# Score tiles off the diagonal by seven half-size products, in one fused graph-layer kernel

## The chip, the cores and the metric

The kernel runs on one core of a Trainium2 chip. Times are device microseconds (us) of one launch. The core has TensorE (PE in the profile, with its weight loads listed as PEld), VectorE (DVE), ScalarE (ACT), GpSimd (POOL) and SyncE (SP). POOL and SP are used here almost only to issue DMA transfers. Each engine has its own queue and takes its instructions in the order of that queue; engines wait for each other through semaphores.

## The reference

Two graph layers on x (4096 rows, 512 columns) with an adjacency matrix adj (4096 x 4096, sparse, symmetric in its pattern). Cut to what matters:

```
ba = maximum(sign(x), 0);  bw = sign(W0)
x  = layernorm(x + relu(adj @ (ba @ bw.T)))          # layer 0

node_att = softmax(x @ node_w, axis=0)               # layer 1
h        = x @ edge_w
e        = h @ h.T                                   # 4096 x 4096 scores, fp32
edge_att = softmax(where(adj > 0, e, -9e15), axis=1)
out      = (adj * (node_att * edge_att)) @ (x @ W1) + bias
x        = layernorm(x + out)
```

The scores e are symmetric, so a tile of e and its transpose are the same numbers. They are products in full fp32.

## The kernel before, in words

P is 128, W is 512. The 4096 rows are eight groups of 512 (index A for the rows of a score tile, B for its columns); h is kept transposed in SBUF as hT (contraction in KD = 4 slices of 128).

**Four stages follow each other.** Layer 0 runs from 0 to about 560 us. h is computed up to 602 us (function `seven`). The score stage runs from 602 to 1063 us. It computes e tile by tile, masks it, takes each row's minimum of the negated scores (VectorE, line 669), the exponentials and their row sums (ScalarE, line 678), and stores the raw scores to HBM in both orientations. From 1063 us to the end the aggregation multiplies the weights that belong to the scores with x (class `Aggregate`, matmuls at line 1326) and finishes with W1 and the layernorm (`Finish`).

**The score stage** is a list `runs` (lines 1636 to 1641). It holds `Single` tiles of 512 x 512, and runs of `Couple`s. There are eight Singles on the diagonal (A equal to B, upper triangle only), four off it, (2,3), (4,5), (0,1) and (6,7), and twelve Couples of 512 x 1024. Together they cover each unordered pair of groups once. `Mirror.turn` (line 707) makes the transposed tile with four TensorE transposes for each block of 128 rows, and ScalarE copies them out of PSUM (line 708).

- A `Single` off the diagonal computes each of its four row blocks with four fp32 matmuls of 512 columns (line 745) into one PSUM bank, which ScalarE copies to SBUF (line 755). There are six such banks in the queue `banks`.
- A `Couple` replaces eight half-size block products by seven, in the way of Strassen and Winograd. It forms sums and differences of quarters of hT on VectorE (`operands`, lines 781 to 813), and products into PSUM (`quad`, line 924), which ScalarE copies (lines 948, 953, 961, 966) or VectorE adds up (line 962). Two of its seven products are again made by seven smaller ones (`second` at line 846, `third` at line 883).

**What sets the order.** In this stage the program text gives a first order: `between()` is called within the tiles, and `tick` takes at most a few deferred jobs from three queues (`turns`: transposes; `stats`: row minima and stores; `exps`: exponentials). Then the tile scheduler is free to reorder instructions on each engine by its own estimates. Only in the aggregation is the order of TensorE, VectorE and ScalarE fixed by hand (`manual_schedule`).

**Buffers.** `free` holds tiles of 128 x 2048 fp32, `free_h` fourteen halves of other such tiles (masks, strips of scores, operands), `free_s` a single tile (slot5; every second Couple's left sums), `lopp` four tiles of 128 x 1024 (a run's right operands, later the left operands of the aggregation). `take` forces deferred jobs when a store is empty.

**The end of the stage.** Seven Singles follow the last run. While they run (`closing`), `early_steps` of the first aggregation block are started between their matmuls: two mask loads, the shifts (line 1095), exponentials (line 1098) and weights (line 1111) of four tiles. After the last Single the differences of these tiles (lines 1120 to 1128) and the first aggregation products follow.

**The end of a run of Couples.** Lines 1710 to 1716 let the last Couple's `third` (four steps, `tail_`) take turns with the last two steps of its second `quad` (`rest_`).

Of the kernel before, what the change touches and what calls it, by code (L numbers as in the profile page):

```python
# [11 lines left out]
F32 = mybir.dt.float32  # L12
# [6 lines left out]
P = 128  # L19
# [10 lines left out]
def kernel(  # L30
# [13 lines left out]
    nc = tc.nc  # L44
    N, D = x.shape
    NB = N // P
    KD = D // P
    W = 512
    NG = N // W
    BG = W // P  # L50
# [675 lines left out]
    class Single:  # L726
# [7 lines left out]
        def main(self, between):  # L734
            A, B = self.A, self.B
            s = Uses(BG + 1 if self.diag else 3 * BG)
            if self.diag:
                self.mirror.t = s
            elif self.stays:
                kept_tiles[A, B] = s.buf  # L740
            for i in range(BG):
                lo = i if self.diag else 0
                pe = banks.popleft()
                for k in range(KD):
                    nc.tensor.matmul(  # L745
                        pe[:, lo * P :],
                        hT[:, k, ts(A * BG + i, P)],
                        hT[:, k, (B * BG + lo) * P : (B + 1) * W],
                        start=(k == 0),
                        stop=(k == KD - 1),  # L750
                    )
                    if k == KD - 1 or k % 2 and not (self.diag and i > 1):
                        between()
                src = s.buf[:, i, :]
                nc.scalar.copy(src[:, lo * P :], pe[:, lo * P :])  # L755
                banks.append(pe)
                turns.append((now[0] + 3, lambda i=i, s=s, src=src: self.mirror.turn(s, src, i)))
                if not self.diag:
                    stats.append((self.here.ready, 1, lambda i=i, s=s, src=src: self.here.row(i, s, src)))

                    if self.stays:
                        continue

                    def store(i=i, s=s, src=src):
                        nc.gpsimd.dma_start(s_d[A][B // 2][:, i, B % 2, :], src)
                        s.used()

                    stats.append((at_once, 0, store))

    class Couple:  # L770
        right, inner_right = {}, {}
# [9 lines left out]
        def operands(self):  # L781
            A, B, h = self.A, self.B, KD // 2
            if B not in Couple.right:
                r11, r12 = (hT[:, :h, ts(c, W)] for c in (B, B + 1))
                r21, r22 = (hT[:, h:, ts(c, W)] for c in (B, B + 1))
                t1, t2, t3, t4 = (lopp.tile([P, h, W], F32, name="right", tag="lop") for _ in range(4))
                nc.vector.tensor_sub(t1, r12, r11)
                nc.vector.tensor_sub(t2, r22, t1)
                nc.vector.tensor_sub(t3, r22, r12)
                nc.vector.tensor_sub(t4, r21, t2)  # L790
                Couple.right[B] = r11, r21, r22, t4, t1, t2, t3
                Couple.inner_right[B] = self.second_right(r21), self.second_right(r22)
            low, high = (hT[:, f : f + h, ts(A, W)].rearrange("p k (q u w) -> p k q u w", u=2, w=P) for f in (0, h))
            l11, l21 = (low[:, :, :, u, :] for u in range(2))
            l12, l22 = (high[:, :, :, u, :] for u in range(2))
            Couple.made[0] += 1
            self.sums = None
            if Couple.made[0] % 2:
                s2, s1, s3, s4 = (rows.tile([P, h, 2, P], F32, name="left", tag="rows") for _ in range(4))
            else:  # L800
                self.sums = Uses(1, free_s)
                s2, s1, s3, s4 = (
                    self.sums.buf[:, n, :].rearrange("p (k q w) -> p k q w", k=h, w=P) for n in range(4)
                )
            nc.vector.tensor_add(s1, l21, l22)
            nc.vector.tensor_sub(s2, s1, l11)
            nc.vector.tensor_sub(s3, l11, l21)
            nc.vector.tensor_sub(s4, l12, s2)
            self.left = l11, l12, s4, l22, s1, s2, s3
            self.inner_sums = Uses(2, free_h)  # L810
            self.inner_left = [self.second_left(l, n) for n, l in enumerate((l12, s4))]
            self.rows11, self.rows12, self.zs = [None] * 2, [None] * 2, [None] * 2
            self.written = [None] * 2
# [456 lines left out]
    class Sums:  # L1270
# [34 lines left out]
        def multiply(self):  # L1305
            r, m = self.unit.r, self.m
            if self.begin:
                lops["lop"] = lopp.tile([P, BG, HD], F32, name="lop")
                nc.sync.dma_start(lops["lop"], lop_d[r][:, m])
            if self.begin and self.ns:  # L1310
                lops["inner"] = lopp.tile([P, BG // 2, 4, P], F32, name="lop2", tag="lop")
                nc.sync.dma_start(lops["inner"], lop2_d[r][:, SPLIT.index(m)])
            if self.ns:
                products = []
                for k, n in enumerate(self.ns):
                    if n in (2, 4, 5, 6):
                        lop = lops["inner"][:, :, n - 3 if n > 2 else 0, :]
                    else:
                        lop = lops["lop"][:, 2 * (n > 0) :, P * (n > 1) :][:, : BG // 2, :P]
                    products.append((self.bank[:, ts(k, W // 2)], lop, self.unit.halves[n], BG // 2))  # L1320
            else:
                products = [(self.bank, lops["lop"][:, :, ts(self.h, P)], self.unit.right(m), BG)]
            start = self.fresh and self.w == W
            for ps, lop, rop, K in products:
                for k in range(K):
                    nc.tensor.matmul(ps, lop[:, k, :], rop[:, k, :], start=start, stop=(k == K - 1), skip_group_check=True)  # L1326
                    start = False
            spend("pe", 0.43 * self.work)
            self.done = clock["pe"]
            if self.keep:  # L1330
                kept.append(self.bank)
# [301 lines left out]
    def couples(B, *As):  # L1633
        return [Couple(A, B) for A in As]

    runs = [Single(2, 2), Single(2, 3), couples(4, 2, 3, 0, 1)]
    runs += [Single(4, 4), Single(4, 5), couples(6, 2, 3, 0, 1, 4, 5)]
    runs += [Single(3, 3), couples(2, 0, 1)]
    every = [c for u in runs if isinstance(u, list) for c in u]
    tail = len(runs)  # L1640
    runs += [Single(0, 0), Single(0, 1), Single(1, 1), Single(6, 6), Single(6, 7), Single(7, 7), Single(5, 5)]
    masks = deque(r for u in runs for c in (u if isinstance(u, list) else [u]) for r in c.masks)
    early_ = deque()

# [20 lines left out]
    for n, u in enumerate(runs):  # L1665
        unit[0] = n
        closing[0] = n >= tail
        if isinstance(u, Single):
            final = []
            u.main(between)  # L1670
            for later in runs[n + 1 : n + 3]:
                if isinstance(later, list) and later[0].left is None:
                    later[0].operands()
            continue
        final = u[-1].mirrors
        quads = [[c.quad(q, between) for q in range(2)] for c in u]
        inners = [c.second(between) for c in u]
        tails = [c.third(between) for c in u]
        for k, c in enumerate(u):
            first, second = quads[k]  # L1680
            rest_ = quads[k - 1][1] if k else None
            next(first)
            if rest_:
                tail_ = tails[k - 1]
                next(tail_)
                next(rest_)
                next(tail_)
            next(first)
            if rest_:
                next(tail_)  # L1690
            next(first)
            if rest_:
                next(rest_)
                next(tail_)
                if u[k - 1].sums:
                    u[k - 1].sums.used()
            next(first)
            inner_ = inners[k]
            next(inner_)
            next(second)  # L1700
            if k + 1 < len(u):
                u[k + 1].operands()
            next(inner_)
            next(first)
            next(inner_)
            next(second)
            next(inner_)
            next(second)
            next(inner_)
        rest_, tail_ = quads[-1][1], tails[-1]  # L1710
        next(tail_)
        next(rest_)
        next(tail_)
        next(rest_)
        next(tail_)
        next(tail_)
        if u[-1].sums:
            u[-1].sums.used()
    while turns or stats or exps:
# [145 lines left out]
```

## Time and profile before

| | us |
|---|---|
| median of 3 runs (1907.35 to 1907.94) | 1907.55 |
| the profiled execution's own time | 1908.56 |
| its span on the core | 1906.8 |
| score stage, first to last L745 matmul | 602.5 to 1062.0 |
| granted TensorE clock over the span | 0.999 of full speed |

An fp32 matmul stands in the trace as two rows, each with a weight load of its own. A row of 128x512 shows 592 ns, but the next one starts 0.43 us later, because matmuls overlap in the pipeline; so one fp32 matmul of 512 columns takes 0.86 us of TensorE. For VectorE and ScalarE too, what a row shows is a little longer than the distance to the next one when they follow each other without a wait. The number behind the bar in a row of the groups is busy time, then the mean duration in ns, then the engine's idle time just before, with what ended it.

### The profile page before, as it was taken

To read this page: it belongs to the slowest core of one execution; us is meant where nothing else is said; L and a number is where in the kernel's file an instruction comes from. 1 tells how busy PE (TensorE), PEld (TensorE's weight loads), DVE (VectorE), ACT (ScalarE), POOL (GpSimd) and SP (SyncE) were. 2 spreads that over 40 slices of the span, in tenths; PEclk is the share of its full clock that TensorE was granted. 3 is DMA by queue.
4 is the path that set the end of the run, shared out by engine and by line. 5 is a ranking of instruction groups with operands and counts; after the bars stand their busy time and mean duration, and the time that the engine had idled before them with its cause. 6 is when DMAs were issued, how large, how long until landed. Compare 5 with 4: busy or idle time off the path is not lost.

```text
span 1906.8 us, 20976 instructions
## 1 busy us (share of the span) xinstructions
PE 1893.8 (99%) x6958; PEld 1247.2 (65%) x6958; DVE 1495.8 (78%) x2357; ACT 1024.9 (54%) x1653; POOL 315.0 (17%) x449
## 2 busy tenths in 40 slices
PE   9999999999999999999999999999999999999998
PEld 6888888888644555565565556666666666656646
DVE  7777677776876588788874887898879988898947
ACT  6433333333212567566777666666676567657732
POOL 0133132231431111111110111111111101110100
PEclk9999999999999999999999999999999999999999
DMA  9889898898585379577784878877877877787731
GB/s 320 303 319 362 303 345 321 326 360 312 178 299 191 139 269 340 187 262 276 280 349 159 318 276 291 293 287 288 278 279 284 299 269 282 265 313 252 282 118 56
DMA packets 143917, 520.97 MB, mean 273 GB/s; under 512 B 15040, under 2 KB 15040, under 8 KB 136128
## 3 DMA queue, kind: packets, MB, share of 16 engines
q1 hardware_dynamic: 64368, 235.43, 36.5%
q0 software_dynamic: 67632, 248.54, 34.0%
q10 hardware_dynamic: 11808, 35.66, 5.1%
q8 instruction: 55, 0.90, 0.2%
q14 instruction: 54, 0.44, 0.1%
HBM read 397.93 MB, written 121.63 MB: 272 GB/s over the span
## 4 chain that ended last, share of the span: by engine, by line
PE 67%; issue 16%; DVE 6%; POOL 5%; DMA 2%; ACT 2%; POOLq 0%; ACTq 0%; SPq 0%; DVEq 0%
PE bank L1326 33%; PE bank L924 10%; PE bank L745 6%; PE seven L101 5%; PE po L1476 4%; PE pt L707 3%; POOL mask_d L340 2%; PE bank L883 2%; PE bank L846 2%; DVE lent L1095 1%; PE acc L253 1%; PE acc L255 1%; POOL x_d L368 1%; DMA xt<-in_x_t_dram 1%; PE bank L1476 1%
## 5 line engine op out<-in xcount | busy, mean ns | idle before, releaser
L1326 PE MATMUL bank<-slot,lop 128*128 128x256 f32 (+1 forms) x1304 | 399.9, 455 | 0.8 <-DMA lop<-lop_d 0.4
L459 PE MATMUL acc<-xw,hi 128*128 128x512 f32 x960 | 376.5, 392 | 0.0
L460 PE MATMUL acc<-xw,lo 128*128 128x512 f32 x960 | 374.3, 390 | 0.2 <-DVE lo L451 0.2
L1326 PE MATMUL bank<-lent,lop 128*128 128x512 f32 (+1 forms) x992 | 369.0, 520 | 1.2 <-DVE lent L1107 1.2
L1326 PEld LDWEIGHTS bank<-slot,lop 128*128 128x128 f32 x1304 | 247.0, 190 | 129.0 <-issue 102.6
L1326 PEld LDWEIGHTS bank<-lent,lop 128*128 128x128 f32 x992 | 188.3, 190 | 154.7 <-issue 139.7
L449 ACT CAST hi<-at 128x1024 fp32r<-128x1024 f32 x120 | 126.5, 1054 | 203.2 <-PE acc L459 149.2
L1337 ACT COPY over<-bank 128x512 f32<-128x512 f32 x200 | 116.1, 586 | 199.4 <-PE bank L1326 195.8
L460 PEld LDWEIGHTS acc<-xw,lo 128*128 128x128 f32 x960 | 180.3, 188 | 37.3 <-DVE lo L451 0.6
L459 PEld LDWEIGHTS acc<-xw,hi 128*128 128x128 f32 x960 | 180.3, 188 | 36.8
L451 DVE TENSOR_TENSOR lo<-at,hi 128x1024 fp32r<-128x1024 f32 x120 | 147.7, 1231 | 66.3 <-ACT hi L449 65.9
L745 PE MATMUL bank<-hT 128*128 128x512 f32 (+3 forms) x384 | 132.3, 486 | 0.0
L678 ACT ACTIVATE line<-line,nmax_c 128x512 f32<-128x512 f32 x160 | 115.0, 726 | 22.9 <-DVE nmax_c L669 22.6
L669 DVE CUSTOM_DVE_ANT_0 line<-lent,slot 128x512 f32<-128x512 bf16 x144 | 93.0, 687 | 40.0 <-ACT slot L755 21.7
L1488 DVE SCALAR_TENSOR_TENSOR xb<-po,f,xb 128x256 f32<-128x256 f32 x84 | 40.3, 481 | 75.0 <-PE po L1476 74.9
L745 PEld LDWEIGHTS bank<-hT 128*128 128x128 f32 x384 | 64.8, 191 | 40.5 <-issue 32.5
L1299 ACT COPY bank<-over 128x512 f32<-128x512 f32 x144 | 86.7, 603 | 0.0
L1095 DVE CUSTOM_DVE_ANT_1 lent<-lent,line 128x2048 f32<-128x2048 f32 x36 | 82.0, 2283 | 0.0
L1098 ACT ACTIVATE lent<-lent 128x2048 f32<-128x2048 f32 x36 | 69.2, 1921 | 19.0 <-DVE lent L1095 19.0
L707 PEld LDWEIGHTS pt<-ident,lent 128*128 128x128 f32 x406 | 50.7, 141 | 35.9 <-issue 24.8
L420 ACT COPY x1T<-pt 128x512 f32<-128x512 f32 x32 | 18.8, 587 | 102.3 <-PE pt L419 102.3
L708 ACT COPY slot<-pt 128x512 f32<-128x512 f32 (+3 forms) x125 | 67.8, 553 | 9.7 <-PE pt L707 9.7
(322 smaller groups left out, 3161.3 us busy)
## 6 DMA issues: line engine op xcount, KB each, us to landing
lop<-lop_d SPq DMA_DIRECT2D x154, 512.0 KB, 4.6
at<-in_adj_t_dram SPq DMA_DIRECT2D x60, 1024.0 KB, 7.1
lent<-in_adj_t_dram POOLq DMA_DIRECT2D x34, 1024.0 KB, 7.6
lent<-s_d POOLq DMA_DIRECT2D x33, 1024.0 KB, 8.2
s_d<-slot POOLq DMA_DIRECT2D x32, 1024.0 KB, 7.7
slot<-in_adj_t_dram POOLq DMA_DIRECT2D x30, 1024.0 KB, 7.9
slot<-s_d POOLq DMA_DIRECT2D x27, 1024.0 KB, 7.9
lent<-in_adj_dram SPq DMA_DIRECT2D x48, 512.0 KB, 6.2
```

The costliest lines, as they stand in the source:

```text
L101: nc.tensor.matmul(banks[bank][q], lop(m, q)[k], rop(m)[k], start=(first and k == 0), stop=(k == K - 1), skip_group_check=not first,)
L449: nc.scalar.copy(hi, aq)
L451: nc.vector.tensor_sub(lo, aq, hi.bitcast(F32))
L459: nc.tensor.matmul(acc, hi[:, c, :], xw[:, kb, :], start=(kb == 0), stop=False)
L460: nc.tensor.matmul(acc, lo[:, c, :], xw[:, kb, :], start=False, stop=(kb == NB - 1))
L678: nc.scalar.activation(line, line, AF.Exp, bias=nmax_c[:, b, c : c + 1], scale=-1.0, accum_out=sum_c[:, b, c : c + 1])
L707: nc.tensor.transpose(pt[:, j, :], src[:, ts(j, P)], ident)
L745: nc.tensor.matmul(pe[:, lo * P :], hT[:, k, ts(A * BG + i, P)], hT[:, k, (B * BG + lo) * P : (B + 1) * W], start=(k == 0), stop=(k == KD ...
L924: nc.tensor.matmul(ps, left[m][:, k, q, :], right[m][:, k, :], start=(first and k == 0), stop=(k == KD // 2 - 1), skip_group_check=not first,)
L1095: pinned[0](nc.vector._custom_dve(TENSOR_ADD_SAT, out=q, in0=q, in1=m, s0=0.0, s1=-HUGE))
L1326: nc.tensor.matmul(ps, lop[:, k, :], rop[:, k, :], start=start, stop=(k == K - 1), skip_group_check=True)
L1337: nc.scalar.copy(self.to(), self.bank[:, : self.w])
```

## The change

Class `Seventh`, a `Single`, takes the four tiles off the diagonal. It halves a 512 x 512 tile in all three directions (rows in blocks of 128 that alternate, columns in halves of 256, contraction in halves of two slices), forms four sums on the left and four on the right with eight VectorE instructions of 128x512, and makes seven products, for each of two q (a pair of row blocks): each product is two fp32 matmuls of 256 columns. For each q they share two banks, (y, z) and (u, v): half y accumulates products 0, 5 and 6, half z products 4 and 2, and u and v hold products 1 and 3. ScalarE copies y after 0, 5 and 6 and z after 4; VectorE adds u, z, y and v to the copies in SBUF.

The operands of a Seventh are formed before the Single ahead of it in the list. For (2,3) the right sums lie in two halves of `free_h`; for the others in two `lopp` tiles. The left sums lie in the one tile of `free_s` until the Seventh is done. Four stores, sixteen transposes and eight rows of statistics for a tile stay as they were.

The last hunk moves the last step of `rest_` (product 3 of the last quad of a run, 2 matmuls of 512 columns) behind the last two steps of `tail_`.

```
--- before.py
+++ after.py
@@ -767,6 +767,93 @@
 
                     stats.append((at_once, 0, store))
 
+    class Seventh(Single):
+
+        def operands(self):
+            h, w = KD // 2, W // 2
+            cols = [slice(self.B * W + n * w, self.B * W + (n + 1) * w) for n in range(2)]
+            (r11, r12), (r21, r22) = ([hT[:, f : f + h, c] for c in cols] for f in (0, h))
+            if self.A == 2:
+                self.keep = [Uses(1, free_h) for _ in range(2)]
+                both = [x.buf for x in self.keep]
+            else:
+                self.keep = []
+                both = [lopp.tile([P, h, W], F32, name="right", tag="lop") for _ in range(2)]
+            t1, t2, t3, t4 = (both[n // 2][:, n % 2, :].rearrange("p (k w) -> p k w", w=w) for n in range(4))
+            nc.vector.tensor_sub(t1, r12, r11)
+            nc.vector.tensor_sub(t2, r22, t1)
+            nc.vector.tensor_sub(t3, r22, r12)
+            nc.vector.tensor_sub(t4, r21, t2)
+            self.right = r11, r21, r22, t4, t1, t2, t3
+            low, high = (hT[:, f : f + h, ts(self.A, W)].rearrange("p k (q u w) -> p k q u w", u=2, w=P) for f in (0, h))
+            l11, l21 = (low[:, :, :, u, :] for u in range(2))
+            l12, l22 = (high[:, :, :, u, :] for u in range(2))
+            self.sums = Uses(1, free_s)
+            s1, s2, s3, s4 = (self.sums.buf[:, n, :].rearrange("p (k q w) -> p k q w", k=h, w=P) for n in range(4))
+            nc.vector.tensor_add(s1, l21, l22)
+            nc.vector.tensor_sub(s2, s1, l11)
+            nc.vector.tensor_sub(s3, l11, l21)
+            nc.vector.tensor_sub(s4, l12, s2)
+            self.left = l11, l12, s4, l22, s1, s2, s3
+
+        def main(self, between):
+            s, w = Uses(3 * BG), W // 2
+            if self.stays:
+                kept_tiles[self.A, self.B] = s.buf
+
+            def multiply(ps, m, q, first=False):
+                for k in range(KD // 2):
+                    nc.tensor.matmul(
+                        ps,
+                        self.left[m][:, k, q, :],
+                        self.right[m][:, k, :],
+                        start=(first and k == 0),
+                        stop=(k == KD // 2 - 1),
+                        skip_group_check=not first,
+                    )
+
+            def written(i):
+                src = s.buf[:, i, :]
+                turns.append((now[0] + 2, lambda: self.mirror.turn(s, src, i)))
+                stats.append((self.here.ready, 1, lambda: self.here.row(i, s, src)))
+                if self.stays:
+                    return
+
+                def store():
+                    nc.gpsimd.dma_start(s_d[self.A][self.B // 2][:, i, self.B % 2, :], src)
+                    s.used()
+
+                stats.append((at_once, 0, store))
+
+            for q in range(2):
+                own = banks.popleft(), banks.popleft()
+                (y, z), (u, v) = ((b[:, :w], b[:, w:]) for b in own)
+                (c11, c12), (c21, c22) = ((s.buf[:, i, :w], s.buf[:, i, w:]) for i in (2 * q, 2 * q + 1))
+                multiply(y, 0, q, True)
+                nc.scalar.copy(c11, y)
+                multiply(z, 4, q)
+                nc.scalar.copy(c22, z)
+                between()
+                multiply(u, 1, q, True)
+                nc.vector.tensor_add(c11, c11, u)
+                multiply(y, 5, q)
+                nc.scalar.copy(c12, y)
+                between()
+                multiply(z, 2, q)
+                nc.vector.tensor_add(c12, c12, z)
+                written(2 * q)
+                multiply(v, 3, q)
+                between()
+                multiply(y, 6, q)
+                nc.scalar.copy(c21, y)
+                nc.vector.tensor_add(c22, c22, y)
+                nc.vector.tensor_add(c21, c21, v)
+                banks.extend(own)
+                written(2 * q + 1)
+                between()
+            for x in (*self.keep, self.sums):
+                x.used()
+
     class Couple:
         right, inner_right = {}, {}
         made = [0]
@@ -1633,12 +1720,12 @@
     def couples(B, *As):
         return [Couple(A, B) for A in As]
 
-    runs = [Single(2, 2), Single(2, 3), couples(4, 2, 3, 0, 1)]
-    runs += [Single(4, 4), Single(4, 5), couples(6, 2, 3, 0, 1, 4, 5)]
+    runs = [Single(2, 2), Seventh(2, 3), couples(4, 2, 3, 0, 1)]
+    runs += [Single(4, 4), Seventh(4, 5), couples(6, 2, 3, 0, 1, 4, 5)]
     runs += [Single(3, 3), couples(2, 0, 1)]
     every = [c for u in runs if isinstance(u, list) for c in u]
     tail = len(runs)
-    runs += [Single(0, 0), Single(0, 1), Single(1, 1), Single(6, 6), Single(6, 7), Single(7, 7), Single(5, 5)]
+    runs += [Single(0, 0), Seventh(0, 1), Single(1, 1), Single(6, 6), Seventh(6, 7), Single(7, 7), Single(5, 5)]
     masks = deque(r for u in runs for c in (u if isinstance(u, list) else [u]) for r in c.masks)
     early_ = deque()
 
@@ -1667,6 +1754,8 @@
         closing[0] = n >= tail
         if isinstance(u, Single):
             final = []
+            if n + 1 < len(runs) and isinstance(runs[n + 1], Seventh):
+                runs[n + 1].operands()
             u.main(between)
             for later in runs[n + 1 : n + 3]:
                 if isinstance(later, list) and later[0].left is None:
@@ -1711,9 +1800,9 @@
         next(tail_)
         next(rest_)
         next(tail_)
-        next(rest_)
         next(tail_)
         next(tail_)
+        next(rest_)
         if u[-1].sums:
             u[-1].sums.used()
     while turns or stats or exps:
```

## The prediction

> **What bounds the kernel now.** I read the page first: busy times, then the slices.
>
> ```profile
> span 1906.8 us, 20976 instructions
> PE 1893.8 (99%) x6958; PEld 1247.2 (65%) x6958; DVE 1495.8 (78%) x2357; ACT 1024.9 (54%) x1653; POOL 315.0 (17%) x449
> PE   9999999999999999999999999999999999999998
> DVE  7777677776876588788874887898879988898947
> ...
> L745 PE MATMUL bank<-hT 128*128 128x512 f32 (+3 forms) x384 | 132.3, 486 | 0.0
> ```
>
> TensorE has no gap in any slice, and the plain tiles' matmuls have no idle before them. A busy share can hide stalls, so I checked the score stage against its work. By the groups with each shape apart, the window 602.4 to 1063 holds 672 rows of 512 columns, 64 of 384, 400 of 256 and 568 of 128. At 0.4295 us for 512 columns (eight rows in 3.44 us) and in proportion below, that is 288.6 + 20.6 + 85.9 + 62.1 = 457 us of a 460.6 us window. So about 3 us are lost in the stage, and only work taken from TensorE, or those 3 us, can shorten it. The waits of TensorE there are two:
>
> ```profile
> PE bank L924 <- ACT lent L961: 0.8, 2, 0.4
> PE pt L707 <- ACT slot L755: 0.4, 1, 0.4
> ```
>
> Next, whether 256 columns cost half of 512. The timeline of TensorE in a Couple:
>
> ```profile
> 779.42 1.88 PE L924 MATMUL bank<-right,left 128*128 128x512 f32 x4
> 781.14 0.59 PE L883 MATMUL bank<-hT,left 128*128 128x256 f32 x2
> 781.57 0.59 PE L883 MATMUL bank<-hT,lent 128*128 128x256 f32 x2
> 782.00 1.88 PE L924 MATMUL bank<-right,slot 128*128 128x512 f32 x4
> ```
>
> Start to start, four rows of 512 take 1.72 us and two rows of 256 take 0.43 us: 0.2147 us a row. The weight load of a row, 190 ns, still fits under it. Last, how busy the helpers are where the last two tiles run, by the windows:
>
> ```profile
> core 0: us, PE busy (x) PEld busy (x) DVE busy (x) ACT busy (x) POOL busy (x), PEclk, DMA share, GB/s
> 985.00:1000.00 15.00, 15.00 (x65) 9.38 (x64) 12.38 (x33) 13.32 (x33) 3.72 (x6) 1.00 1.02 406
> 1000.00:1020.00 20.00, 20.00 (x77) 11.52 (x76) 7.13 (x24) 15.21 (x41) 0.78 (x1) 1.00 0.70 261
> 1020.00:1040.00 20.00, 20.00 (x73) 11.29 (x72) 10.84 (x24) 14.55 (x32) 1.80 (x3) 1.00 0.31 109
> 1040.00:1064.00 24.00, 23.61 (x98) 14.75 (x97) 18.21 (x35) 18.59 (x43) 3.80 (x6) 1.00 0.50 175
> ```
>
> VectorE has room from 1000 on; ScalarE is three quarters full.
>
> **What the Trainium skill says.** (1) "TensorE: Matmul & The Clock Gate", section "Back-to-back issue gap", gives 518 cycles for 512 columns and 262 for 256: in proportion, with almost no fixed part. The trace agrees (0.4295 and 0.2147 us a row). (2) "Perfetto Trace Analysis", section "Optimizing Scalar/DVE Operations", says that a profiled duration overlaps the next instruction by the write acknowledgement, so the distance between starts is the price. The trace agrees: VectorE's 128x512 sums show 0.69 us and follow each other every 0.60, those of 128x256 show 0.42 and follow every 0.335. (3) The same page, section "Matmuls", advises that independent groups rotate through banks so that copying one out overlaps the next. A Single does this with six banks. A Seventh accumulates on in the bank just copied, so it has less of that cover. No row of before shows that pattern with products this short.
>
> **The change, part by part.** *TensorE, certain.* A tile had 16 fp32 matmuls of 512 columns, 32 rows x 0.4295 = 13.74 us. It gets 2 x 7 x 2 = 28 of 256, 56 rows x 0.2147 = 12.03 us. Saved: 1.72 us a tile, 6.87 us for four. Transposes stay.
>
> *VectorE, added.* Eight operand sums x 0.60 = 4.8 us and eight additions of 128x256 x 0.335 = 2.7 us: 7.5 us a tile. Row minima stay. *ScalarE:* eight copies of 256 (one follows another's start after 0.26 us) for four of 512 (0.47): +0.2 us a tile.
>
> What hides this: (2,3) forms its sums at 603 to 608, where the queue of the changed program puts them behind the last h sums; everything behind, up to the first row minimum at 609.9, comes 4.8 us later, and VectorE's gaps from 614 to 633 (0.54 + 1.35 + 1.95 + 3.17 + 3.17 + 5.32 = 15.5 us) take that and the 2.7. TensorE reaches the tile at about 611.5, after the sums are there. For (0,1) and (6,7), VectorE has about 23 us of gaps from 978 to 1028 for 12.4 us of new work, and 10.7 us from 1028 to 1063 for 2.7. A gap of this kind is one behind a ScalarE copy:
>
> ```profile
> 1002.13 0.69 DVE L669 CUSTOM_DVE_ANT_0 line<-lent,lent 128x512 f32<-128x512 bf16 x1 [2.47 <-ACT lent L755]
> 1005.21 0.69 DVE L669 CUSTOM_DVE_ANT_0 line<-lent,lent 128x512 f32<-128x512 bf16 x1 [2.38 <-ACT lent L755]
> ```
>
> *New waits on TensorE.* In the changed program's queue z's product 4, products 5 and 2 wait for ScalarE's copy of their bank, product 3 (bank of u) and product 6 (bank of z) for VectorE's addition: ten such waits a tile, each with about one product (0.86 us) of other work before it. Everything on TensorE is queued behind them. The least price of a hand-over is 0.17 us of drain (0.59 shown less 0.43), a copy of 0.38 or an addition of 0.42, and about 0.1 for the semaphore: 0.65 to 0.7 us, under 0.86. It stalls when an exponential (0.72 us) or a row minimum (0.61) stands ahead. I walked the queues by these durations. (0,1), y0 at 993.2: product 1 ends at 995.2; VectorE's queue has its c11 sum behind the operand sums, the last Couple's sums and seven row minima, at about 995.8, done 996.1; product 3 is due at 996.2. Product 4's copy is late by 0.1, product 5's by 0.2. In (4,5) I find 0.3 at the second q's product 2, behind three exponentials, and 0.3 at the last transposes, which wait for the v addition behind a 1.14 us right sum of the next run. (2,3): 0.2. (6,7): 0.1; its two shifts and 1.92 us exponentials stand where there is slack. Sum 1.2 us; about six more places had no more than 0.1 of margin, so I take 1.6 us. Bounds: 0 (all hidden), and 0.4 us at each of 40, 16 us, if each met half an exponential.
>
> *Other queues.* VectorE's left sums of the Couple after (2,3), in slot5, wait for products of the Seventh; row minima wait behind, all inside its slack. On SP, a mask load issued at about 606 now waits for (2,3) to give up its two halves (about 625), and its mask is used near 656; the next load waited until 656.7 already. On POOL, the second block's load into slot5, issued at 985.96, must wait for (6,7) to end (about 1041); its shift ran at 1090, so some 40 us of cover remain for a load of 8 us. Its place in the queue is behind stores that wait for the same tile.
>
> *The held product.* Two matmuls of 512 move, nothing is added. The scheduler of this stage already fills between the last small products (at most 0.1 us lost per wait at 980 to 983), so I take 0. Bounds: +0.4 (TensorE's whole idle at L924 is 0.8 over two waits) and, if the last strip's transposes had to be waited for, -0.4 at each of three runs.
>
> *What is late next.* The first aggregation product is tight:
>
> ```profile
> 1060.71 2.49 DVE L1111 SCALAR_TENSOR_TENSOR lent<-lent,lent 128x512 f32<-128x512 f32 x4
> ...
> 1063.05 7.04 PE L1326 MATMUL bank<-lent,lop 128*128 128x512 f32 x16
> ```
>
> Of the four parts its first needs the one ending at 1061.3, so it had 1.7 us. In the changed queue the third shift stands behind (6,7)'s additions, two row minima after its last one. From (6,7)'s end: 2.2 us to that shift, 13.6 of VectorE work to the weights, 0.6 for the first part: 16.4, and TensorE arrives at 17.9 (1063.05 less 1045.1). It still fits, by 1.5 us. The third product's operand had 3.5 us.
>
> **Sum.** 6.87 - 1.6 + 0 = 5.3 us. The aggregation is TensorE's without gaps, so it moves up as it is. Profiled execution: span 1906.8 - 5.3 = 1901.5. The median is 0.75 above that span (the profiled execution's own 1908.56 is 1.8 above it): 1902.3 us, or -0.28%.
>
> **The rivals.** A, the forecast: stalls under 3 us, 3.8 to 7.2 us gained, 1900.3 to 1903.8. For it: the Couples do the same hand-overs on a fuller VectorE with about 3 us lost in 460. Against: their covers are mostly 1.72 us.
>
> B, *the short cover eats it*: the waits behind exponentials last 0.13 us on average, 40 x 0.13 = 5.2, gain 1.7: 1905.9 us. For it: ScalarE at 13.3 of 15 us before 1000, in-order. Against: the walk.
>
> C, *VectorE becomes the bound at the end of the stage*, slower. Place: the queue from 978 to the first aggregation product. New there: 15.1 us, and TensorE comes 3.4 us earlier. If only f us of the 34 us of gaps can be used (because each is a wait for a copy that comes no earlier), the first product is late by 15.1 + 3.4 - 1.7 - f. It turns the change into a loss when f is under 9.9. With f = 6 it loses 10.8 against 6.9: 1911.5 us. Against it: the walk uses the 5.4 us of gaps before 991 in full, and 4.5 of the 28 behind them are then enough.
>
> D, *the change does not do what it says*: the cost of 256 columns would have to exceed 0.245 us a row for no gain; the row above says 0.2147, and the built program has 28 matmuls for 16. I give it nothing; the held product alone is nil as above.
>
> **Chances.** A 0.68, B 0.22, C 0.10. A measurement of this kernel can tell about 0.2%, 3.8 us, from no change. A counts as faster, B as the same, C mostly as slower: 0.69, 0.22, 0.09. The range 1900.2 to 1907.0 takes in A with all stalls hidden (1900.7) and nearly all of B, and leaves out C: about 0.86 held. A alone is 1900.3 to 1903.8.
>
> **What will show it.** TensorE rows up by 96 to 7054; each Seventh, first to last product with its transposes, about 1.5 us shorter; idle before its rows under 0.5 us a tile, from ScalarE and VectorE; the first aggregation product at about 1058, without idle over 0.5. Wrong if TensorE's waits in the four tiles sum to over 3 us (B), or if the first aggregation rows wait for VectorE (C). The h stage and the aggregation's length (1063.05 to the end) should be unchanged within 0.5 us.

## The result and the profile after

The changed kernel takes 1904.44 us (median of 20 runs, 1903.03 to 1908.48), the kernel before 1907.58 us beside it (20 runs, 1906.90 to 1909.85). The ratio is 0.9983 with a 95% interval of 0.9977 to 0.9989, so 3.1 us are gained, 0.17%: under the 0.2% that I had set as what can be told from no change, though the interval holds no loss. The forecast was 1902.3. A later run of the changed kernel on another chip gave 1904.41 against 1907.95, 3.5 us. The two profiled executions differ by more, 4.6 us (1908.56, 1.0 over its median, against 1903.96, 0.5 under); I use the traces for where time lies, and the medians for how much the change is worth.

The page after, in the lines that answer to those shown of before (span, busy time of an engine with its number of instructions, busy tenths in 40 slices, the group of plain tile matmuls):

```profile
span 1902.2 us, 21262 instructions
PE 1890.8 (99%) x7054; PEld 1263.4 (66%) x7054; DVE 1527.5 (80%) x2421; ACT 1024.6 (54%) x1669; POOL 314.1 (17%) x449
PE   9999999999999999999999999999999999999998
DVE  7777677776877689888896887898879988898947
...
L745 PE MATMUL bank<-hT 128*128 128x512 f32 (+3 forms) x256 | 75.1, 433 | 0.0
```

TensorE has the 96 rows more that were forecast and 3 us less of busy time; VectorE has 32 us more. TensorE still looks full everywhere. The view of TensorE's waits in the score stage of the changed kernel (engine, what waited, for whom: us in total, times, longest) has a single line:

```profile
PE bank L1413 <- DVE lent L1198: 0.2, 1, 0.2
```

That is the first aggregation product. Nothing here tells of a stall in a Seventh. The stretches that answer to those of before:

```profile
core 0: us, PE busy (x) PEld busy (x) DVE busy (x) ACT busy (x) POOL busy (x), PEclk, DMA share, GB/s
985.00:1000.00 15.00, 14.93 (x82) 12.11 (x80) 14.40 (x38) 14.49 (x41) 2.09 (x3) 1.00 1.03 385
1000.00:1020.00 20.00, 19.98 (x86) 12.97 (x85) 11.67 (x36) 15.71 (x44) 0.00 (x0) 1.00 0.47 148
1020.00:1040.00 20.00, 19.91 (x99) 15.73 (x98) 12.95 (x30) 14.55 (x33) 2.35 (x4) 1.00 0.39 132
```

VectorE's gaps after 1000 took the new work, as the walk had it. At the stage's last step TensorE now waits for VectorE, but only for 0.19 us. The shifts' weights and the first aggregation product in the timeline:

```profile
1058.16 1.90 DVE L1198 SCALAR_TENSOR_TENSOR lent<-lent,lent 128x512 f32<-128x512 f32 x3
...
1058.91 1.12 PE L1413 MATMUL bank<-lent,lop 128*128 128x512 f32 x2 [0.19 <-DVE lent L1198]
```

**Where the time went.** Busy shares can't say it, so I charged each group of rows in TensorE's timeline with the time from its start to the start of the next group; a stall then counts to the group before it. The span fell by 4.6 us: 0.4 in the h stage before (the stage begins at 602.09 for 602.48), 3.76 in the score stage (456.82 for 460.58, first plain row to first aggregation row), and 0.45 in the aggregation, which is not changed. In the score stage:

| charged to, us | before | after |
|---|---|---|
| rows of Singles (L745) | 124.1 | 69.2 |
| rows of Sevenths (L806) | 0 | 51.7 |
| rows of Couples | 280.7 | 279.9 |
| transposes (L707) | 54.9 | 55.0 |
| eight rows of `panel` (L990, then L1077) | 0.9 | 1.0 |

The four plain tiles were worth 54.9 us, which is 4 x 13.74: they lost nothing to waits. Four Sevenths without a stall would be 4 x 56 x 0.2147 = 48.1. They take 51.7: **3.6 us of the 6.87 are lost inside the tiles** (1.05 in (2,3), 0.78 in (4,5), 0.82 in (0,1), 0.91 in (6,7)).

The weight loads show why the view of TensorE's own waits is nearly silent: here the blocked instructions stand at their weight loads. A row of 256 columns is shown for 0.38 us, although the next one may start after 0.21, and this overhang covers most of a wait. What is left as idle time before the matmuls of the Sevenths is 0.07 to 0.12 us at four places, too short for that view to list. The waits of weight loads in the score stage of the changed kernel, the largest of the Sevenths:

```profile
PEld bank L806 <- DVE slot L843: 1.3, 4, 0.5
PEld bank L806 <- ACT slot L835: 1.3, 4, 0.5
PEld bank L806 <- ACT slot L833: 1.1, 4, 0.4
PEld bank L806 <- ACT slot L840: 0.8, 2, 0.5
```

All nine lines of this kind come to 6.1 us over 19 waits, 4.1 of it for ScalarE's copies and 2.0 for VectorE's additions. It is not all lost, since a weight load that comes early gains nothing. One hand-over (a product, the copy that reads its bank, the next product into that bank) in (2,3) in full, from product 4 (`lent,slot`) over its copy (L835) to product 5 (`lent,slot`) in the same bank; a row gives start, duration, engine, line, operands, and in brackets how long the engine was idle before:

```profile
612.57 1.10 PE L806 MATMUL bank<-lent,slot 128*128 128x256 f32 x4
613.51 0.59 PE L806 MATMUL bank<-hT 128*128 128x256 f32 x2
613.71 0.37 ACT L835 COPY slot<-bank 128x256 f32<-128x256 f32 x1 [0.94 <-PE bank L806]
613.94 0.27 PE L707 MATMUL pt<-ident,slot 128*128 128x128 f32 x1
614.13 0.73 PEld L806 LDWEIGHTS bank<-lent,slot 128*128 128x128 f32 x4 [0.27 <-ACT slot L835]
614.13 1.13 PE L806 MATMUL bank<-lent,slot 128*128 128x256 f32 x4
...
615.10 0.59 PE L806 MATMUL bank<-hT 128*128 128x256 f32 x2
```

The row behind product 4 starts at 613.51; ScalarE, idle before, starts its copy 0.20 us later; the next weight load starts at 614.13. So a hand-over with a free ScalarE takes 0.62 us. Between them stood two rows of product 1 and a transpose, 0.43 + 0.11 = 0.54 us: 0.08 short. Then the first weight load starts together with its row and has nothing to hide behind: the four rows show 1.13 us where unblocked ones show 1.03 (the first row 483 ns instead of 379). I call these 0.10 us the reload. Together 0.18 us, and not one bracket of idle time on a PE row.

**The reloads are 1.6 us of the 3.6.** In the changed kernel 16 of the 224 rows of Sevenths are longer in this way (over 400 ns, thirteen of them 483), and what they show over 379 ns sums to 1.57 us. One group of rows (shortest, median and longest in ns):

```profile
L806 PE MATMUL bank<-hT,slot x32: 379/379/483, 616.2 to 1038.1; 128*128 128x256 f32 x32
```

The other 2.0 us are waiting. 1.2 of them stand at six places where the copy or addition came late because its engine had been at another instruction until then, 0.25 at one place where VectorE was idle and the product before had only just passed; the rest are smaller pieces. The trace of before has the reload too, after its waits at L924: these four rows of 512 columns show 1.98 us, where the timeline in the prediction has 1.88.

```profile
728.64 1.98 PE L924 MATMUL bank<-right,hT 128*128 128x512 f32 x4 [0.41 <-ACT lent L961]
```

### The profile page after: what moved, and what is told of

It is laid out like the page before. It is cut to its first block, busy times and chain, and to the rows that moved or that the text cites. A ratio compares the mean times of both kernels' runs of the same rounds, so it can differ in the third digit from the quotient of the medians.

```text
span 1902.2 us, 21262 instructions
## 1 busy us (share of the span) xinstructions
PE 1890.8 (99%) x7054; PEld 1263.4 (66%) x7054; DVE 1527.5 (80%) x2421; ACT 1024.6 (54%) x1669; POOL 314.1 (17%) x449
## 4 chain that ended last, share of the span: by engine, by line
PE 89%; DVE 7%; ACT 2%; DMA 1%; issue 1%; ACTq 0%; SPq 0%; DVEq 0%
PE bank L1413 33%; PE acc L460 11%; PE acc L459 11%; PE bank L1011 11%; PE seven L101 5%; PE po L1563 4%; PE pt L707 3%; PE bank L806 2%; PE bank L970 2%; PE bank L933 2%; PE bank L745 2%; DVE lent L1182 1%; PE pt L419 1%; DVE slot L1182 1%; PE acc L253 1%
## 5 line engine op out<-in xcount | busy, mean ns | idle before, releaser
L1413 PE MATMUL bank<-lent,lop 128*128 128x256 f32 (+1 forms) x1368 | 433.0, 466 | 1.1 <-DVE lent L1194 0.7
L1413 PEld LDWEIGHTS bank<-lent,lop 128*128 128x128 f32 x1368 | 259.3, 190 | 146.1 <-issue 119.9
L1413 PE MATMUL bank<-slot,lop 128*128 128x512 f32 (+1 forms) x928 | 335.4, 508 | 0.4 <-DMA lop<-lop_d 0.2
L1413 PEld LDWEIGHTS bank<-slot,lop 128*128 128x128 f32 x928 | 176.0, 190 | 136.8 <-issue 121.3
L678 ACT ACTIVATE line<-line,nmax_c 128x512 f32<-128x512 f32 x160 | 115.2, 726 | 22.4 <-DVE nmax_c L669 22.0
L707 PEld LDWEIGHTS pt<-ident,lent 128*128 128x128 f32 x406 | 50.9, 141 | 36.6 <-issue 24.2
L745 PE MATMUL bank<-hT 128*128 128x512 f32 (+3 forms) x256 | 75.1, 433 | 0.0
L1182 DVE CUSTOM_DVE_ANT_1 lent<-lent,line 128x2048 f32<-128x2048 f32 x32 | 73.0, 2283 | 1.1 <-DMA lent<-s_d 1.1
L1188 ACT ACTIVATE slot<-slot 128x2048 f32<-128x2048 f32 x35 | 67.3, 1924 | 10.8 <-DMA slot<-in_adj_t_dram 10.8
L1182 DVE CUSTOM_DVE_ANT_1 slot<-slot,line 128x2048 f32<-128x2048 f32 x32 | 73.1, 2284 | 0.0
```

Source lines behind the costliest of these rows:

```text
L678: nc.scalar.activation(line, line, AF.Exp, bias=nmax_c[:, b, c : c + 1], scale=-1.0, accum_out=sum_c[:, b, c : c + 1])
L707: nc.tensor.transpose(pt[:, j, :], src[:, ts(j, P)], ident)
L745: nc.tensor.matmul(pe[:, lo * P :], hT[:, k, ts(A * BG + i, P)], hT[:, k, (B * BG + lo) * P : (B + 1) * W], start=(k == 0), stop=(k == KD ...
L1182: pinned[0](nc.vector._custom_dve(TENSOR_ADD_SAT, out=q, in0=q, in1=m, s0=0.0, s1=-HUGE))
```

## The experiments

Each is the changed kernel but for what is said. "Stage" is the score stage, "rows" the time charged to the rows of the four Sevenths, and "long" the number of these rows over 400 ns, all as above, in the profiled execution.

| kernel | median, us | before beside it | ratio, 95% interval | stage | rows | long |
|---|---|---|---|---|---|---|
| changed kernel | 1904.44 | 1907.58 | 0.9983, 0.9977 to 0.9989 | 456.82 | 51.7 | 16 |
| e1 Sevenths only | 1904.31 | 1907.92 | 0.9981, 0.9973 to 0.9989 | 456.80 | 50.8 | 14 |
| e2 held product only | 1907.27 | 1907.92 | 0.9996, 0.9987 to 1.0004 | 460.54 | none | none |
| e3 q in turns | 1902.98 | 1907.92 | 0.9975, 0.9965 to 0.9985 | 455.72 | 50.6 | 7 |
| e4 no copies | 1902.66 | 1907.92 | 0.9973, 0.9962 to 0.9984 | 455.35 | 49.8 | 5 |
| e6 other pairing | 1902.90 | 1908.18 | 0.9972, 0.9962 to 0.9982 | 455.69 | 50.4 | 13 |
| e7 turns and pairing | 1901.60 | 1908.18 | 0.9963, 0.9951 to 0.9976 | 454.08 | 49.0 | 1 |
| e8 sums twice | 1903.59 | 1908.18 | 0.9979, 0.9971 to 0.9987 | 456.08 | 50.4 | 13 |
| e9 e7, not held | 1902.59 | 1907.95 | 0.9970, 0.9959 to 0.9982 | 454.96 | 48.8 | 3 |
| e10 changed, again | 1904.41 | 1907.95 | 0.9979, 0.9971 to 0.9988 | 456.68 | 51.6 | 16 |

My theory, before the runs: what is missing went into the hand-overs within the tiles. The rivals: VectorE's larger load took it, or the held product costs something. The intervals of e1, e3, e4, e6, e8 and e9 overlap that of the changed kernel, so for these the rows have to say what the medians only suggest.

**e1 and e2, one part alone.** e1 puts the end of a run of Couples back, e2 puts only that hunk into the kernel before:

```
-        next(tail_)
-        next(tail_)
         next(rest_)
+        next(tail_)
+        next(tail_)
```

> The four tiles by seven products, the last product of a run not held back. Theory 1 (each such tile keeps only about 0.6 of its 1.72 us because its hand-overs between TensorE, ScalarE and VectorE are longer than the work put between them; the trace of the change shows 2.3 us kept in the four tiles and 1.1 us over three run ends): 2.3 us under the kernel before, and 0.5 to 1 us slower than the full change. Rival (the held product is worth nothing, as I had forecast, and the 1.1 us are chance): equal to the full change, 3.1 us under the kernel before.

> Only the held product; the tiles stay plain. Theory 1: 0.5 to 1 us faster than the kernel before, 1906.6 to 1907.1. Rival (held product worth nothing): the same within 0.3 us. A loss would say that the tiles alone gained more than 3.1 us.

Measured: e1 gains 3.6 us, as much as the full change, so the rival fits and the theory's 2.3 does not. e2 gains 0.65; that is what the theory gave, but its interval holds no change. The net gain is that of the Sevenths. The hunk does do something, though: see e9.

**e3, the two q in turns.** Product by product, first q then second, on four banks:

```
-            for q in range(2):
+            def steps(q):
                 own = banks.popleft(), banks.popleft()
...
                 multiply(y, 0, q, True)
                 nc.scalar.copy(c11, y)
+                yield
                 multiply(z, 4, q)
...
+            for _ in zip(*(steps(q) for q in range(2))):
+                pass
```

> The full change, with the two q of a tile taken in turn, product by product, in four banks: about two products (1.72 us) instead of one lie between a product and the one that waits for its copy or addition. Theory 1 (cover too short): most of the 4.6 us lost in the four tiles come back, 2 to 4 us under the full change, 1900.5 to 1902.5. Rival 2 (ScalarE's and VectorE's queues are too full at these tiles, whatever the order): the same as the full change within 1 us. Rival 3 (four banks at once leave too few for the tiles beside it): slower than the full change.

Measured: 4.9 us gained, some 1.5 more than the changed kernel; rows 50.6. The direction is right and the size is below what was expected (the 4.6 us lost that the expectation starts from are 3.6 by the table above). Its trace says why: in this order product 4 still follows product 0 of its bank with one product between, and product 2 follows product 5 so; of the waits left, the longest are again for those copies (1.6 us in three waits at the copy after product 5).

**e4, no copies.** The three copies inside the tile are left out, and VectorE writes where it added:

```
                 multiply(y, 0, q, True)
-                nc.scalar.copy(c11, y)
                 multiply(z, 4, q)
-                nc.scalar.copy(c22, z)
...
-                nc.vector.tensor_add(c11, c11, u)
+                nc.vector.tensor_copy(c11, u)
```

> The full change with three of ScalarE's four copies of each q left out and VectorE's additions turned into copies that write alone, so the values of these four tiles leave out some of their products. TensorE's work is unchanged, three of its five waits per q are gone. Theory 1: 2 to 3 us under the full change, about 1902. Rival 2 (VectorE's load or its late results hold TensorE): within 0.7 us of the full change, since VectorE has as many instructions as before.

Measured: 5.3 us gained, rows 49.8. So the copies cost 1.9 us of the 3.6, of which 1.05 are reloads (5 long rows for 16). VectorE's writes no longer wait for a copy either, so this is not the price of ScalarE's time alone. The weight load waits that are left stand at VectorE's writes out of the banks (2.9 us in six waits).

**e6, the other pairing.** The halves of a bank are (y, v) and (u, z), and the order is 0, 1, 5, 4, 3, 2, 6, so that each reuse has exactly one product ahead of it in the text. With this pairing four of the five waits of each q are left: product 6 no longer waits for a reader of its own.

```
-                (y, z), (u, v) = ((b[:, :w], b[:, w:]) for b in own)
+                (y, v), (u, z) = ((b[:, :w], b[:, w:]) for b in own)
```

> The changed kernel with the other pairing and order alone, one q after the other: each reuse has one product (0.86 us) ahead of it, against a hand-over of about 0.73 us with the weight load that isn't hidden. Theory 1: the waits that found nothing ahead of them shrink, those that find ScalarE or VectorE at other work stay: rows of the four tiles 50.0 to 51.0 us, time 1902.8 to 1903.8. Theory 1 with the price of my prediction (under 0.86 us, so one product covers it): 1901 to 1902.3. Rival (VectorE's load or pushed out work): 1904 to 1905, as the changed kernel.

Measured: rows 50.4, time 1902.9: the first of the three. With one product of cover at each place, 2.3 us stay lost, 1.2 of it in reloads. The largest line of its weight load waits is for the copy after product 5:

```profile
PEld bank L806 <- ACT slot L838: 1.6, 4, 0.5
```

One of these waits, in (4,5), in the timeline of e6: product 5's rows pass by about 746.6, the copy (L838) starts when an exponential (L678) is through, and the weight load waits 0.53 us:

```profile
746.36 0.79 ACT L678 ACTIVATE line<-line,nmax_c 128x512 f32<-128x512 f32 x1
...
747.08 0.43 ACT L838 COPY slot<-bank 128x256 f32<-128x256 f32 x1
...
747.56 0.73 PEld L806 LDWEIGHTS bank<-right,hT 128*128 128x128 f32 x4 [0.53 <-ACT slot L838]
```

One product would cover the 0.62 us of a copy that starts at once, but here it did not cover one behind an exponential.

**e7, both.** The pairing of e6 with the turns of e3, so three products (2.58 us) stand before each reuse.

> The changed kernel with both turns of q taken product by product and the halves of a bank paired otherwise, (y, v) and (u, z), with the order y0, u1, y5, z4, v3, z2, y6: a product that reuses a half waits for a copy or an addition that has three other products (12 rows of 0.2147 us, 2.58 us) ahead of it, against nothing or one product in the changed kernel. Theory 1 (what is missing of the 6.87 us went into the hand-overs within the four tiles): the four tiles' rows take 48.1 to 49.3 us in all, start to start, against 51.7 in the changed kernel, and the time is 1900.5 to 1901.8. Rival (what is missing is lost to VectorE's larger load or to work that was pushed out of the tiles, whatever the order within them): no better than the turn by turn kernel with the old pairing, 1902.5 to 1904.5.

Measured: rows 49.0, time 1901.6, stage shorter than before by 6.5 us: within what the theory gave, and the best of all. Its interval ends at 0.9976, and that of the changed kernel begins at 0.9977 (0.9971 in e10). Rows of (2,3), (0,1) and (6,7) take 12.1 us each, with nothing lost. All weight load waits of its Sevenths that the view lists:

```profile
PEld bank L806 <- DVE slot L836: 0.7, 1, 0.7
```

That one is in (4,5), where the addition of u stands in VectorE's queue behind the operand sums of the next Couples (L918 to L931); the trace of e7 there:

```profile
746.89 0.28 DVE L930 TENSOR_TENSOR lent<-left 128x128 f32<-128x128 f32 x1
747.09 0.29 DVE L929 TENSOR_TENSOR lent<-lent,left 128x128 f32<-128x128 f32 x1
747.29 0.41 DVE L836 TENSOR_TENSOR slot<-slot,bank 128x256 f32<-128x256 f32 x1
...
747.76 1.13 PE L806 MATMUL bank<-right,slot 128*128 128x256 f32 x4 [0.29 <-DVE slot L836]
```

**e8, the operand sums twice.** Each of the four tiles' eight sums is made two times into the same buffer:

```
             nc.vector.tensor_sub(t4, r21, t2)
+            nc.vector.tensor_sub(t1, r12, r11)
+            nc.vector.tensor_sub(t2, r22, t1)
+            nc.vector.tensor_sub(t3, r22, r12)
+            nc.vector.tensor_sub(t4, r21, t2)
```

> The changed kernel with each of the four tiles' eight operand sums on VectorE made twice into the same buffer: 32 additions of 0.685 us, 21.9 us more of VectorE. Theory 1 (VectorE has room in these stages, and what is missing went into hand-overs): 1904.4 to 1905.6, at most 0.3 us a tile lost. Rival (VectorE's load is what ate the gain: 21.9 us of sums cost some 3 to 4 us, so as much again is lost): 1907.5 to 1911.

Measured: 4.6 us gained, no less than without (3.1 and 3.5), although the page has 16.7 us more of VectorE's busy time (1544.2 for 1527.5). The time, 1903.59, lies under the theory's lower end, and the rows take 1.2 us less than in the changed kernel. The scheduler had put TensorE's rows in another order in three of the four tiles (in (4,5) with products of the next Couples between those of the Seventh), so e8 changes more than VectorE's load; what each part did is open. In (6,7), where TensorE's order is the same, the rows take 12.6 us for 12.9. The stretch around (2,3) in the changed kernel, then in e8:

```profile
612.00:640.00 28.00, 27.87 (x107) 17.78 (x106) 19.96 (x61) 16.70 (x43) 4.19 (x7) 1.00 0.44 163
```

```profile
612.00:640.00 28.00, 27.98 (x111) 18.38 (x110) 25.00 (x71) 16.97 (x44) 4.19 (x7) 1.00 0.45 166
```

So the larger load did not lengthen this kernel, and that rival, which had 1907.5 or more, falls. What can cost is one addition at a bad place in VectorE's queue, as in e7. e1 and e8 also show that the rows move by 0.8 to 1.2 us with an order that was not meant to change; the 1.0 and 1.3 of e3 and e6 are no larger than that, and the 2.7 of e7 is.

**e9 and e10.** e9 is e7 with the end of a run of Couples as before, e10 the changed kernel beside it.

> The best version so far (both turns of q taken product by product, the halves paired (y, v) and (u, z)), with the last products of a run of couples back in their old order. Theory (the held product is worth nothing): 1901 to 1902, as with it. Rival (it is worth the 0.4 us at each of three runs that the hand-over is short of cover there): 1902.4 to 1903.2. An order that costs less without it: 1900 to 1900.8.

> The changed kernel itself, beside the best version on one chip: 1903.5 to 1905, so 2 to 3.3 us over the other, if the 2.7 us of rows that the four tiles lose less there are what separates the two; under 1 us if the lower medians of the later kernels were the chip's.

Measured: e10 is as the changed kernel was, and 1.8 us over e9 beside it, so the chip doesn't make the gain of turns and pairing; that is a little less than the 2 forecast, for a best version that e9 is not. e9 lies 1.0 us over e7 in the medians, with intervals that overlap, so the times alone don't separate them. The traces do show what the held product does. TensorE's waits in e9 have a line that the kernel before and e1 have too, with other line numbers:

```profile
PE bank L1021 <- ACT lent L1058: 0.8, 2, 0.4
```

In e2, in the changed kernel and in e7 that line is gone: two stalls of 0.4 us, at the ends of the first two runs. The time charged to Couples falls with the hunk in each of the three pairs (before to e2 by 0.7, e1 to changed by 0.8, e9 to e7 by 1.0). But the stage is shorter by it only from e9 to e7 (0.88). From before to e2 the rows of Singles take 0.6 more: it stands before two groups of transposes, 0.18 us at 1004 and 0.45 at 1018. From e1 to the changed kernel the rows of the Sevenths take 0.8 more, about half of it in (4,5) and (0,1), where TensorE's order differs between the two, and the rest in (6,7), where it does not. Why it is given back I could not settle.

## Why the prediction was right or wrong

The sign and the place were right, and the time lay in the range; the size was too large: 5.3 us forecast, 3.1 to 3.5 measured, which is below case A's 3.8 and above B's 1.7. That the time lay in the range says little for the mechanism, since the range took in nearly all of B as well.

- **TensorE's saving, 6.87 us: right.** A row of 256 still costs 0.2147 us, the plain tiles had 54.9 us to give, and the three undisturbed tiles of e7 take 12.1 us for a forecast of 12.03. The proportion rests on the trace alone: the section of "TensorE: Matmul & The Clock Gate" that the prediction cites ("Back-to-back issue gap") gives its cycles for an isolated matmul, and for a stream of them 81 ns at 128 columns and 131 at 512, which is not in proportion.
- **The term that was too small: the stalls, 1.6 us forecast and 3.6 found.** Of the 2.0 us more, 1.6 are reloads. The prediction's price of a hand-over (drain, copy, semaphore) was right at 0.65 to 0.7 us for 0.62 measured, but it put nothing for the weight load behind it, on the ground that the "weight load of a row, 190 ns, still fits under it". That holds for a row that isn't blocked. Each blocked one took 0.10 us more, sixteen times, and the trace of before had shown it at L924.
- **The waits proper: 1.6 forecast, 2.0 found; near in sum, less so by place.** By tile they are 0.4 in (2,3), 0.5 in (4,5), 0.5 in (0,1) and 0.5 in (6,7), where the walk had 0.2, 0.6, 0.3 and 0.1, and 0.4 with no place. 1.2 of the 2.0 stood behind exponentials, copies and sums, which is B's reason; with the reloads the whole, 3.6, lies between my 1.6 and B's 5.2.
- **The cover: not as the prediction said.** It gave each wait "about one product (0.86 us) of other work before it". In the text, products 4 and 2 follow a copy of their bank with no product between, products 5 and 6 with one, product 3 with two. In (2,3) the scheduler put half of product 1 and two transposes (0.64 us) before product 4, which left 0.54 before product 5. The cover decides how many hand-overs are blocked, and so both the waits and the reloads: with three products (e7) 0.9 us are lost and one row is long. With one product at each place (e6) it is 2.3, but how much of the 1.3 us between that and the changed kernel is the cover's is not shown: one wait fewer for each q and another order came with it.
- **"Wrong if TensorE's waits in the four tiles sum to over 3 us (B)": by the distance between starts they do, 3.6 us with the reloads.** The view in which I meant to read it doesn't show them, and the sign "idle before its rows under 0.5 us a tile" came true with about 0.1 a tile and says nothing. A tile became 0.7 to 0.9 us shorter in its rows, not 1.5.
- **The held product, 0: right in the net of before and e2, for a wrong reason.** The prediction took half of the 0.8 us at L924 as the most that could be gained, and nothing as the gain, because at 980 to 983 at most 0.1 us was lost per wait. That is the end of the third run. The two stalls of 0.41 us stand at the ends of the first two, at 728.64 and 914.47, and the hunk takes both away. That the gain is given back elsewhere in e2 was luck for the forecast.
- **C, VectorE as the bound: fell.** The first aggregation product came at 1058.91 with 0.19 us of idle; the forecast was about 1058 with under 0.5. So the margin of 1.5 us that the prediction worked out was gone. But in e7 TensorE reaches this product at 1056.10, 2.8 us earlier, without a wait for VectorE, and e8 shows room for as many sums again.
- **SP, POOL, the aggregation: as forecast.** SP's mask load waited until 623.6 (forecast 625), POOL issued the load into slot5 at 1040.74 (forecast 1041). From the first aggregation row to the end it took 843.74 us before and 843.28 after.
- **One sum is off.** 568 rows of 128 columns at a quarter of 0.4295 us are 61.0 us, not 62.1. So 4.5 us of the score stage before were not covered by rows at this rate, and not about 3, which weakens a reason given for A.

The chances put 0.69 on a gain over 0.2% and 0.22 on none that can be told; the second came. With the cover that the prediction had assumed, in e6, the gain was 5.3 us, the number forecast; but its stalls were 2.3 us and not 1.6, so that this agreement is in part chance.

## What to carry to other kernels

Before a product accumulates on in a bank that another engine must read first, count what stands between them in TensorE's queue: here 0.62 us were needed when the reader was free, and one product of 0.86 us was too little where an exponential of 0.72 us stood ahead of the copy. Price a blocked product with its reload, 0.10 us here, and not with the wait alone. Letting two independent halves of the work take turns, and pairing in a bank what is used far apart, brought the loss in four tiles from 3.6 to 0.9 us with the same number of matmuls, copies and additions. The turns are the rotation through banks that the Trainium skill advises ("Perfetto Trace Analysis", section "Matmuls"), and e7 bears them out together with the pairing. Look for such losses by the distance between starts, by the weight loads' waits and by rows that are longer than their group's median, and don't trust the idle time of the matmuls alone.

## What the runs showed of the hardware

- The waits of these fp32 products show at the weight load and hardly at the matmul: in the changed kernel 6.1 us of weight load waits in the Sevenths stand beside 0.4 us of idle time before their matmuls. A longer wait draws more: one of 0.69 us in e7 stands beside 0.29 us of it.
- After such a wait the first weight load (190 ns) starts together with its row and is not hidden: the first row of 256 columns shows up to 483 ns where others show 379, and one of 512 columns 697 where others show 592 (before, L924). In the changed kernel this is 1.6 us of the 3.6 lost.
- With ScalarE free, a bank that its copy of 128x256 reads was given back 0.62 us after the start of the row behind the product (611.92 to 612.54 and 613.51 to 614.13 in the changed kernel), though the copy itself shows 0.37.
- Another 16.7 us of VectorE's work, on an engine that is busy for 80% of the span, did not lengthen the kernel (e8, in which the order of TensorE's rows changed too).
